# Post-norm attention and ternary feed-forward block on one core: the last seven tiles of the weight quantizer are quantized behind the projections, one a step, in other buffers

## The chip, the core and the metric

The kernel runs on one core of a Trainium2 chip. Its engines are PE (matrix multiply, with PEld for the loading of its weights), DVE (vector), ACT (scalar), POOL (GpSimd) and SP (which here only issues DMAs). Each engine works through its own list of instructions in order; semaphores tie the lists together. The metric is device time in microseconds. The kernel before takes 661.32 us (median of three runs, 660.82 to 663.54).

## The reference

Four sequences of 512 rows, model width 512, 16 query heads of 32 columns that share one key head and one value head, then a feed-forward part of hidden width 1408 whose three weights are first reduced to the values -1, 0 and 1:

```python
x = _layernorm(x + attn(x, Wq, bq, Wk, bk, Wv, bv, Wo, bo))   # rotary q, k; softmax; shared k, v
x = _layernorm(x + ffn(x, w1, w2, w3))

def _quantize(w):
    gamma = jnp.mean(jnp.abs(w))
    return jnp.clip(jnp.round(w / (gamma + EPS)), -1.0, 1.0)
def _bitlinear(x, w):
    return jnp.matmul(x, _quantize(w).T)
def ffn(x, w1, w2, w3):
    return _bitlinear(jax.nn.sigmoid(_bitlinear(x, w1)) * _bitlinear(x, w2), w3)
```

Everything is float32.

## The kernel before

**Steps.** The program is written as 64 steps, n = 0 to 63: sequence b = n // 16, column chunk c of 128 (four heads), row chunk t of 128 keys. A step emits, for its four heads, eight score matmuls (`ps`: four from `qT` and `kT`, four that add the negated row maxima from `negm`), two exponentials on ACT (`es`), and the weighing of the step before (`acc`). For b > 0 POOL adds up the exponentials (`total`, four additions for each step with t > 0). Seven steps ahead (`LEAD = 7`) the row maxima of a later head are found: PE makes `pmax`, DVE reduces it to `maxima`; `spread` turns a chunk's maxima into `negm` by two small DMAs of SP (`rows<-m`, then two of `negm<-rows`).

**Filler.** What else PE has to do is drawn into the steps by `fill.draw`: the projections of the next sequences (`project_in`: `pk`, `pq`), the output projection (`project_out`: `po`, then the transposes `pt`, which DVE splits into `y`), and the feed-forward part (`feed_forward`: `gu`, `hw`, `h`, `po`). As long as projections are left (`batches[-1].done < NC`, up to step 25) a step takes the first branch of the loop, after that the second one.

**Quantizing.** `quantized()` is a generator of 66 jobs; `quantize(k)` runs k of them. The matrices w1, w2, w3 have eleven tiles of 128x512 each. A first pass over a matrix sums absolute values on ACT (`junk`), a second one writes the ternary tile: ACT makes `sgn` (bfloat16), DVE makes the result in place (`raw<-raw,hi,sgn`), POOL stores it to DRAM (`kept`, in the profile `w<-raw`). POOL also issues the loads (`raw<-in_wf`), four jobs ahead; a store is issued two jobs behind its job. Jobs 55 to 65 are the second pass over w3. Three jobs stand in each of the seven leading steps, two in each of steps 0 to 15, and one or two in each step from 16 on, so that job 65 falls in step 25.

**Buffers.** `raw` lies in the rings `wg` (4 buffers, even jobs) and `wd` (5 buffers, odd jobs) of `wp`. The feed-forward part later loads its weights into the same rings (`load_weight`, loads `wg<-w` and `wd<-w` on SP), and takes a buffer when its last user is through, a store to DRAM included. `xT`, the transposed input, has a ring of 6 buffers in `work`. `sgn` lies in the ring `th` (2 buffers, later that of the gate's `th`) up to step 16, and after it in `rot_a`, a single buffer.

**Order.** Every engine call goes through `tc.keep_in_program_order`, so each engine's list is in the order in which the steps emit. SP's list holds the weights' loads, the heads' loads (`qr<-qp`), and the small DMAs for `negm` and for the denominators (`parts`, `few`, `flat`, `rden`), one behind the other.

Of the kernel before, what the change touches and what calls it, by code (L numbers as in the profile page):

```python
# [10 lines left out]
F32 = mybir.dt.float32  # L11
F32R = mybir.dt.float32r
BF16 = mybir.dt.bfloat16
# [7 lines left out]
P = 128  # L21
# [7 lines left out]
def postln_block(  # L29
# [22 lines left out]
    W = 512  # L52
# [4 lines left out]
    work = ctx.enter_context(tc.tile_pool(name="work", bufs=2))  # L57
    xp = ctx.enter_context(tc.tile_pool(name="xp", bufs=8))
    hp = ctx.enter_context(tc.tile_pool(name="hp", bufs=8))
    wp = ctx.enter_context(tc.tile_pool(name="wp", bufs=4))  # L60
# [16 lines left out]
    act, dve, pool = InOrder(nc.scalar), InOrder(nc.vector), InOrder(nc.gpsimd)  # L77

    def mm(out, lhsT, rhs, start, stop):
        pin(nc.tensor.matmul(out, lhsT=lhsT, rhs=rhs, start=start, stop=stop))  # L80

    def move(out, in_):
        pin(nc.sync.dma_start(out=out, in_=in_))
# [70 lines left out]


    kept = [[dram.tile([P, W], F32R, name=f"w{m}_{f}") for f in range(NF)] for m in range(3)]

    def quantized():

        order = ((0, False), (1, False), (0, True), (2, False), (1, True), (2, True))
        jobs = [(m, last, f) for m, last in order for f in range(NF)]

        means = {}
        for n, (m, last) in enumerate(order):
            if not last:
                for k, step in ((2, 0), (6, 1), (10, 2)):
                    means[(n + 1) * NF + k] = (m, step)
        raws, part, row, pg, hi, waiting = {}, {}, {}, {}, {}, []  # L170

        def load(k):
            if k < len(jobs):
                m, _, f = jobs[k]

                tag, bufs = ("wd", 5) if k % 2 else ("wg", 4)
                raws[k] = wp.tile([P, W], F32, tag=tag, name="raw", bufs=bufs)
                pool.dma_start(out=raws[k], in_=wf[m, f])

        def mean(m, step):  # L180
            if step == 0:
                row[m] = small.tile([P, 1], F32, tag="row", name="row")
                dve.tensor_reduce(row[m], part[m], AX.X, ALU.add)
            elif step == 1:
                pg[m] = ps_mm.tile([P, 1], F32, tag="mm", name="pg")
                mm(pg[m], ones, row[m], True, True)
                gamma = small.tile([P, 1], F32, tag="gamma", name="gamma")
                act.activation(gamma, pg[m], AF.Identity, scale=1.0 / (NF * W * P), bias=eps_q)
                row[m] = gamma
            else:  # L190
                hi[m] = small.tile([P, 1], F32, tag="hi", name="hi")
                act.mul(hi[m], row[m], 0.5)

        AHEAD = 4
        for k in range(AHEAD):
            load(k)
        for k, (m, last, f) in enumerate(jobs):
            load(k + AHEAD)
            if k in means:
                mean(*means[k])  # L200
            raw = raws.pop(k)
            if not last:
                if f == 0:
                    part[m] = small.tile([P, NF], F32, tag="part", name="part", bufs=3)
                junk = work.tile([P, W], BF16, tag="th", name="junk")
                act.activation(junk, raw, AF.Abs, accum_out=part[m][:, f : f + 1])
            else:
                if now > PER:

                    sgn = work.tile([P, W], BF16, tag="rot_a", name="sgn", bufs=1)  # L210
                else:
                    sgn = work.tile([P, W], BF16, tag="th", name="sgn")
                act.activation(sgn, raw, AF.Sign, bias=hi[m])
                dve.scalar_tensor_tensor(raw, raw, hi[m], sgn, ALU.is_gt, ALU.min)
                waiting.append((kept[m][f], raw))
            if len(waiting) > 2 or k + 1 == len(jobs):
                for w, q in waiting[: 1 if k + 1 < len(jobs) else 3]:
                    pool.dma_start(out=w.bitcast(F32), in_=q)
                del waiting[:1]
            yield  # L220

# [124 lines left out]
    def load_q(b, c):  # L346
        q = batches[b].q[c] = work.tile([P, T], F32, tag="qT", name="qT", bufs=3)
        move(q, batches[b].qd[c][0])
# [65 lines left out]
    def scores(b, c, t):  # L414
        s = batches[b]
        pss = []
        for j in range(2):
            ps = ps_sc.tile([P, 2, T], F32, tag="sc", name="ps")
            pss.append(ps)
            for i in range(2):  # L420
                rows = ts(2 * j + i, HD)
                mm(ps[:, i, :], s.kT[rows, ts(t, P)], s.q[c][rows, :], True, False)
        for j, ps in enumerate(pss):
            for i in range(2):
                rows = slice(HD * (2 * j + i), HD * (2 * j + i) + 2)
                mm(ps[:, i, :], ones_r[rows, :], s.negm[c][rows, :], False, True)
        es = []
        for j, ps in enumerate(pss):
            e = esp.tile([P, 2, T], F32, tag="es", name="es")
            act.activation(e, ps, AF.Exp, scale=SCALE)  # L430
            es.append(e)
        if b > 0:

            if t == 0:
                s.first = es
            elif t == 1:
                s.total = [work.tile([P, 2, T], F32, tag=f"total{j}", name="total", bufs=1) for j in range(2)]
                for j in range(2):
                    for i in range(2):
                        pool.tensor_tensor(  # L440
                            s.total[j][:, i, :], s.first[j][:, i, :], es[j][:, i, :], ALU.add
                        )
            else:
                for j in range(2):
                    for i in range(2):
                        pool.tensor_tensor(
                            s.total[j][:, i, :], s.total[j][:, i, :], es[j][:, i, :], ALU.add
                        )
        return es
# [130 lines left out]
        dve.tensor_tensor(tail, whole, head.bitcast(F32), ALU.subtract)  # L580

    def load_weight(m, f):
        tag, bufs = ("wd", 5) if m == 2 else ("wg", 4)
        w = wp.tile([P, W], F32R, tag=tag, name=tag, bufs=bufs)
        move(w.bitcast(F32), kept[m][f].bitcast(F32))
        return w
# [200 lines left out]
    def quantize(n):  # L787
        for _ in range(n):
            next(weights, None)

    steps = [(b, c, t) for b in range(B) for c in range(NC) for t in range(NT)]
    PER = NC * NT
# [5 lines left out]
    now = -1  # L798
# [3 lines left out]
    def due():  # L802

        nonlocal slot
        slot += 1
        for entry in list(late):
            if slot >= entry[0] and next(entry[1], "end") == "end":
                late.remove(entry)

    def begin_middle():  # L810
        late.extend(middle)
        middle.clear()
# [31 lines left out]
    def feed(b):  # L844
        fill.urgent.append(project_out(b))
        yield
# [18 lines left out]
    for n, (b, c, t) in enumerate(steps):  # L865
        now = n
        pace = (1.8, 3.8, 4.8, 4.6)[b]
        if t == 1 and PER <= n + NT - 1 < len(steps):
            load_q(*steps[n + NT - 1][:2])
        es = scores(b, c, t)  # L870
        if last is not None:
            weigh(*last)
        if last is not None and last[0] == 0:
            count(*last)
        last = (b, c, t, es)
        if n == NC * NT // 2:

            late.append((slot, load_x(0)))
        if t == NT - 1:
            begin = slot + 3  # L880
            late.append((begin, normalize(b, c)))
            if c == NC - 1:
                late.append((begin + 7, feed(b)))
                if b > 0:
                    late.append((slot + 6, load_x(b)))
        if batches[-1].done < NC:

            if b == 0:
                find_maxima(n + LEAD, 0, 1)
                begin_middle()  # L890
                due()
                find_maxima(n + LEAD, 2, 3)
            else:
                find_maxima(n + LEAD, 0)
                find_maxima(n + LEAD, 1, 2)
                find_maxima(n + LEAD, 3)
                begin_middle()
                due()
            quantize(1)
            fill.draw(pace)  # L900
            quantize(1 if b == 0 or n % 3 == 0 else 0)
        else:
            find_maxima(n + LEAD, 0)
            fill.draw(0.4 * pace)
            find_maxima(n + LEAD, 1, 2)
            begin_middle()
            due()
            fill.draw(0.3 * pace, True)
            find_maxima(n + LEAD, 3)
            fill.draw(0.3 * pace)  # L910
        due()
    weigh(*last)
    now = len(steps)
# [68 lines left out]
```

## Time and profile before

| what | us |
|---|---|
| median of the runs (lowest, highest) | 661.32 (660.82, 663.54) |
| the profiled execution's own time | 659.87 |
| its span, first to last instruction | 658.1 |
| PE busy | 635.4 (97%) |
| DVE busy | 440.3 (67%) |
| POOL busy | 327.4 (50%) |
| ACT busy | 282.6 (43%) |

The profile is of one execution. "Busy" is the time in which an engine has an instruction under way; the idle time in front of an instruction is put down to what released it. The chain of waits follows the work that ended last back to its start. The table by stretch gives each engine's busy time between two moments of the span, and the timeline gives the instructions of one engine in order of time; in it a number of instructions in a row is merged (x8), and a bracket tells the idle time before them and what ended it. In the span, step 16 begins at about 149 us, step 26 at 224.0, step 27 at 232.7, step 28 at 238.4, step 29 at 245.4, step 30 at 252.6, step 31 at 259.7, step 32 at 266.7 and step 33 at 275.6.

### The profile page before, as it was taken

The page shows a single profiled execution, that of the slowest core. Times are in us where ns is not written, and L with a number is a line of the kernel's source. Part 1 is how long each engine was busy: PE and PEld are TensorE (multiplying, and loading weights), DVE is VectorE, ACT ScalarE, POOL GpSimd, SP SyncE. Part 2 cuts the span into 40 slices and gives each one's busy share as a digit, 9 for nine tenths or more (in the row PEclk, how much of TensorE's full clock was granted, in tenths as well). Part 3 has the DMA queues.
Part 4 walks back from the last instruction along what each step waited for, and adds up shares of the span by engine and source line. Part 5 has one row for each costly group of instructions (what it writes and reads, how often), then busy time and mean ns, then how long its engine had stood idle before and what let it go on. Part 6 is the DMA issues. An engine that isn't in the chain of part 4 may idle for free.

```text
span 658.1 us, 9358 instructions
## 1 busy us (share of the span) xinstructions
PE 635.4 (97%) x3194; PEld 357.2 (54%) x3194; DVE 440.3 (67%) x629; ACT 282.6 (43%) x441; POOL 327.4 (50%) x416
## 2 busy tenths in 40 slices
PE   8999999999999999999999899999998999999995
PEld 5233333443333356665555566655555685778884
DVE  3987765787998977676666867667536544364335
ACT  2474656564454645333244354333454521234213
POOL 2434344545998766467666275576575703202000
PEclk9999999999999999999999999999999999999998
DMA  8946669788676286464132457541131473237531
GB/s 265 316 164 209 204 194 273 230 254 259 171 238 205 89 250 190 136 191 147 46 106 77 117 163 219 158 143 44 55 116 52 145 236 120 81 112 229 175 109 64
DMA packets 60671, 107.78 MB, mean 164 GB/s; under 512 B 14592, under 2 KB 15360, under 8 KB 60624
## 3 DMA queue, kind: packets, MB, share of 16 engines
q1 hardware_dynamic: 51984, 80.57, 40.2%
q0 software_dynamic: 7920, 25.96, 12.3%
q10 hardware_dynamic: 720, 0.66, 0.4%
q8 instruction: 25, 0.41, 0.3%
q14 instruction: 22, 0.18, 0.1%
HBM read 84.06 MB, written 23.10 MB: 163 GB/s over the span
## 4 chain that ended last, share of the span: by engine, by line
PE 85%; DVE 9%; ACT 4%; issue 2%; POOL 0%; DVEq 0%; ACTq 0%; POOLq 0%
PE gu L80 24%; PE po L80 19%; PE ps L80 13%; PE pmax L80 9%; PE acc L80 7%; PE pq L80 7%; DVE maxima L75 3%; ACT es L75 2%; PE den L80 2%; PE pk L80 2%; DVE part L75 1%; DVE xt L75 1%; DVE y L75 1%; DVE st L75 1%; PE warm L80 1%
## 5 line engine op out<-in xcount | busy, mean ns | idle before, releaser
L75 DVE TENSOR_REDUCE maxima<-pmax 128x1 f32<-128x512 f32 (+1 forms) x169 | 157.8, 955 | 69.9 <-PE pmax L80 69.7
L75 ACT ACTIVATE es<-ps 128x1024 f32<-128x1024 f32 x128 | 124.2, 1021 | 117.6 <-PE ps L80 116.7
L80 PE MATMUL gu<-y,wg 128*128 128x512 f32 x704 | 171.6, 393 | 0.1
L80 PEld LDWEIGHTS gu<-y,wg 128*128 128x128 f32 x704 | 131.7, 188 | 33.7 <-issue 4.9
L75 POOL TENSOR_TENSOR total<-total,es 128x512 f32<-128x512 f32 x96 | 125.2, 1336 | 38.5 <-ACT es L75 38.3
L80 PE MATMUL po<-wd,h 128*128 128x512 f32 x352 | 86.5, 394 | 3.3 <-DVE y L75 2.9
L75 POOL TENSOR_TENSOR total<-es 128x512 f32<-128x512 f32 x48 | 60.9, 1302 | 52.5 <-ACT es L75 52.5
L80 PE MATMUL pmax<-kr,qr 128*128 128x512 f32 x192 | 74.7, 452 | 3.2 <-DVE maxima L75 1.0
L80 PEld LDWEIGHTS po<-wd,h 128*128 128x128 f32 x352 | 65.1, 188 | 20.8 <-DVE y L75 4.6
L75 ACT CAST h<-hw 128x512 fp32r<-128x512 f32 x44 | 27.3, 620 | 103.0 <-DVE hw L75 103.0
L80 PE MATMUL acc<-es,v 128*32 128x512 f32 x512 | 68.2, 605 | 0.0
L80 PEld LDWEIGHTS pmax<-kr,qr 128*128 128x128 f32 x192 | 34.6, 188 | 55.9 <-issue 17.0
L75 DVE SCALAR_TENSOR_TENSOR hw<-th,gu 128x512 f32<-128x512 f32 x44 | 30.2, 686 | 44.3 <-PE gu L80 43.1
L80 PE MATMUL po<-wo_sb,ctxT 128*128 128x512 f32 x128 | 58.8, 592 | 0.0
L75 DVE TENSOR_TENSOR h<-hw,h 128x512 fp32r<-128x512 f32 x44 | 44.2, 1005 | 21.7 <-ACT h L75 21.4
L80 PE MATMUL ps<-negm,ones_r 2*128 2x512 f32 x256 | 58.7, 788 | 0.0
L75 DVE SCALAR_TENSOR_TENSOR xt<-po,xt 128x512 f32<-128x512 f32 x48 | 32.8, 684 | 37.0 <-PE po L80 37.0
L80 PE MATMUL ps<-qT,kT 32*128 32x512 f32 x384 | 56.3, 640 | 0.0
L75 POOL DMA_DIRECT2D raw<-in_wf x66 | 36.0, 548 | 38.1 <-DMA w<-raw 27.2
L80 PE MATMUL pq<-xT,wq_sb 128*128 128x512 f32 x112 | 53.1, 602 | 0.9 <-ACT v L75 0.9
L75 ACT ACTIVATE th<-gu 128x512 f32<-128x512 f32 x44 | 26.3, 597 | 49.9 <-PE gu L80 49.8
L80 PEld LDWEIGHTS po<-wo_sb,ctxT 128*128 128x128 f32 x128 | 24.1, 189 | 21.2 <-issue 19.2
(99 smaller groups left out, 640.2 us busy)
## 6 DMA issues: line engine op xcount, KB each, us to landing
wg<-w SPq DMA_DIRECT2D x88, 256.0 KB
raw<-in_wf POOLq DMA_DIRECT2D x66, 256.0 KB, 4.6
qr<-qp SPq DMA_DIRECT2D x96, 128.0 KB
wd<-w SPq DMA_DIRECT2D x44, 256.0 KB
w<-raw POOLq DMA_DIRECT2D x33, 256.0 KB, 4.6
qp<-q SPq DMA_DIRECT2D x48, 128.0 KB
rden<-flat SPq DMA_DIRECT2D x64, 64.0 KB
xt<-in_x SPq DMA_DIRECT2D x16, 256.0 KB
```

What stands on the lines that cost most here:

```text
L75: return lambda *args, **kw: pin(getattr(self.engine, name)(*args, **kw))
L80: pin(nc.tensor.matmul(out, lhsT=lhsT, rhs=rhs, start=start, stop=stop))
```

## The change

The last seven jobs (59 to 65) get buffers of the ring `xT`, which the projections leave one by one, and their loads are issued two jobs ahead in place of four. While projections are left, sequence 1 quantizes one tile in every second step; after them, one tile in each step. The signs always lie in the ring `th`. `load_weight` makes sure that a tile was stored before its load is emitted.

```diff
+    LATE = 7
+    stored = set()
...
-                tag, bufs = ("wd", 5) if k % 2 else ("wg", 4)
-                raws[k] = wp.tile([P, W], F32, tag=tag, name="raw", bufs=bufs)
+                if k >= len(jobs) - LATE:
+                    raws[k] = work.tile([P, W], F32, tag="xT", name="raw", bufs=6)
+                else:
+                    tag, bufs = ("wd", 5) if k % 2 else ("wg", 4)
+                    raws[k] = wp.tile([P, W], F32, tag=tag, name="raw", bufs=bufs)
...
-            load(k + AHEAD)
+            if k + AHEAD < len(jobs) - LATE:
+                load(k + AHEAD)
+            elif k + 2 >= len(jobs) - LATE:
+                load(k + 2)
...
-                if now > PER:
-
-                    sgn = work.tile([P, W], BF16, tag="rot_a", name="sgn", bufs=1)
-                else:
-                    sgn = work.tile([P, W], BF16, tag="th", name="sgn")
+                sgn = work.tile([P, W], BF16, tag="th", name="sgn")
...
     def load_weight(m, f):
+        while (m, f) not in stored:
+            quantize(1)
...
                 begin_middle()
                 due()
-            quantize(1)
+            quantize(1 if b == 0 or n % 2 == 0 else 0)
             fill.draw(pace)
-            quantize(1 if b == 0 or n % 3 == 0 else 0)
+            quantize(1 if b == 0 else 0)
         else:
...
             begin_middle()
             due()
+            quantize(1)
             fill.draw(0.3 * pace, True)
```

The stored tiles are also entered in `stored` where POOL's store is emitted.

More of the change, by code (lines that the diff above doesn't have):

```diff
@@ L207, in quantized @@
             else:
-                if now > PER:
-                    sgn = work.tile([P, W], BF16, tag="rot_a", name="sgn", bufs=1)
-                else:
-                    sgn = work.tile([P, W], BF16, tag="th", name="sgn")
+                sgn = work.tile([P, W], BF16, tag="th", name="sgn")
                 act.activation(sgn, raw, AF.Sign, bias=hi[m])
                 dve.scalar_tensor_tensor(raw, raw, hi[m], sgn, ALU.is_gt, ALU.min)
-                waiting.append((kept[m][f], raw))
+                waiting.append((m, f, raw))
             if len(waiting) > 2 or k + 1 == len(jobs):
-                for w, q in waiting[: 1 if k + 1 < len(jobs) else 3]:
-                    pool.dma_start(out=w.bitcast(F32), in_=q)
+                for m, f, q in waiting[: 1 if k + 1 < len(jobs) else 3]:
+                    pool.dma_start(out=kept[m][f].bitcast(F32), in_=q)
+                    stored.add((m, f))
                 del waiting[:1]
```

## The prediction

> **What bounds the kernel now.** I read the page first: busy times, and the chain that ended last.
>
> ```profile
> PE 635.4 (97%) x3194; PEld 357.2 (54%) x3194; DVE 440.3 (67%) x629; ACT 282.6 (43%) x441; POOL 327.4 (50%) x416
> PE 85%; DVE 9%; ACT 4%; issue 2%; POOL 0%; DVEq 0%; ACTq 0%; POOLq 0%
> ```
>
> PE is the bound, so a gain can only come out of its 22.7 us of idle time (658.1 - 635.4). The table by stretch shows how much of that lies where the change works. Columns: length, then busy time (and instructions) of PE, PEld, DVE, ACT, POOL, then granted clock, DMA share, GB/s.
>
> ```profile
> 187.30:202.00 14.70, 14.32 (x66) 5.62 (x65) 14.27 (x18) 6.09 (x8) 13.46 (x15) 1.00 0.88 290
> 224.00:232.70 8.70, 6.39 (x41) 3.27 (x40) 7.94 (x14) 5.49 (x9) 8.68 (x9) 1.00 0.60 178
> 232.70:238.40 5.70, 5.58 (x37) 2.81 (x36) 4.37 (x7) 2.70 (x4) 5.63 (x6) 1.00 0.84 267
> 245.40:252.60 7.20, 7.20 (x42) 4.49 (x41) 6.02 (x8) 3.24 (x5) 4.59 (x4) 1.00 1.02 293
> ```
>
> Up to step 25 DVE is full (14.27 of 14.70), yet PE idles 0.4 us in two steps. Only step 26 (224.0 to 232.7) loses time: 2.3 us. From step 27 on PE is full and DVE has 15 to 50% to spare. PE's timeline (start, length, engine, line, operation, in brackets the idle time before it and what ended it) gives the two waits of step 26, and the two matmul groups of step 28 that matter below:
>
> ```profile
> 229.20 0.66 PE L86 MATMUL pt<-ident,xt 128*128 128x128 f32 x4 [1.13 <-DVE q L75]
> 232.13 0.66 PE L86 MATMUL pt<-ident,xt 128*128 128x128 f32 x4 [1.07 <-DVE y L75]
> 238.36 1.14 PE L80 MATMUL ps<-qT,kT 32*128 32x512 f32 x8
> 238.92 0.81 PE L80 MATMUL ps<-negm,ones_r 2*128 2x512 f32 x4
> ```
>
> Last, the queues that the moved jobs pass, SP's and POOL's timelines:
>
> ```profile
> 232.36 1.51 SPq L83 DMA_DIRECT2D wg<-w  x3
> 233.92 1.08 SPq L83 DMA_DIRECT2D negm<-rows  x2
> 242.07 0.34 SPq L83 DMA_DIRECT2D wg<-w  x1
> ...
> 220.83 4.96 POOL L75 TENSOR_TENSOR total<-es 128x512 f32<-128x512 f32 x4 [2.88 <-ACT es L75]
> 225.75 1.74 POOL L75 TENSOR_TENSOR q<-q,q 128x512 fp32r<-128x512 f32 x1
> 227.43 1.63 POOL L75 DMA_DIRECT2D w<-raw  x3
> 229.07 4.96 POOL L75 TENSOR_TENSOR total<-total,es 128x512 f32<-128x512 f32 x4
> ```
>
> The third `wg<-w` (tile 1 of w1) starts at about 233.4, and `negm` for step 28 is directly behind it.
>
> **What moves.** Set side by side, the two programs have the same lists on PE and SP. DVE, ACT and POOL have the same work in another order: 13 jobs (53 to 65) in steps 16 to 25 become five there and eight (58 to 65) one a step in steps 26 to 33. A job is a sign (ACT 0.72), a `raw` operation (DVE) and two DMA issues (POOL 0.54 and 0.55).
>
> **Taken from steps 17 to 25.** Eight `raw` operations: 13 of them in this stage have a median of 1.22 us, so 9.8 us of DVE, and 8 x 1.09 = 8.7 us of POOL. PE's idle time from 155 to 215 is 1.5 us (60.0 - 58.5), put down to `es` and `v`, which stay; I take 0. In step 26 the wait of 1.13 goes: two `raw` (0.75 and 1.14, with 0.69 of waiting for a sign) no longer stand ahead of `q`, which ends some 2 us earlier. Late next is `y`: job 58's `raw` now stands ahead of the second `y`, against POOL's additions of step 26 (from 227.0 on). It costs 0.75 to 2.96 (the longest `raw`), so the fourth `pt` comes between 1 us sooner and 1 us later than 232.13. ACT's 8.8 us of waiting for the single sign buffer also goes; no PE wait hangs on it. Whatever is won here is lost in step 28, as follows.
>
> **The new wait.** Buffers decide it. Job 58 keeps a buffer of `wg` until its store, and jobs 54 and 56 were held longer too; so the third weight load, tile 1 of w1, gets the buffer of job 56 and waits for that job's store to land. Before, it waited for the store of job 62, issued at about 217. Now job 56's store is emitted with job 58, in step 26. In POOL's list it stands behind: `total` of step 25 (220.83 to 225.8), `q` (1.26, to 227.05), `total` of step 26 (4.96, to 232.0), `q` (1.26, to 233.3), one load's issue (0.56): 233.9. Landing from issue: 4.0 for the single store at 210 (DMA share 0.68), 2.5 in the quietest place (217), 6.0 in the fullest (139). I take 4.0, since the share of the stretch is between: 237.9. SP goes on at 238.0 in place of 233.4, 4.6 late. The second `negm` load starts at 234.45 + 4.6 = 239.05. Its landing: 1.85 (`flat` at 205.12 to `rden` at 206.97) and 2.45 (`rows` at 257.41 to `negm` at 259.86) are SP's waits for such small transfers; at most 3.9, since before it was issued by 235.0 and in use at 238.92. I take 2.45: 241.5, against 238.92: **+2.6**. Ends: 2.5 and 1.85 give 239.3, +0.4; 6.0 and 3.9 give 244.9, +6.0.
>
> The page "DMA: Bandwidth & Descriptors" of the Trainium skill, section "Anatomy of one DMA — SWDGE (gpsimd) path", fits 2.0 us plus bytes over 436 GB/s, which for 256 KB would be an estimated 2.6 us, against the 4.0 measured here; by it the wait would be 1.2 us.
>
> Behind `negm` on SP are `flat`, `qw`, `qp`, `qr`, `rden` and the next weight, tile 1 of w2: issued at 242.07 + 4.1 = 246.2 (SP stood idle for 0.5 at 235.0), there 3.7 later by the first weight (232.36 to 236.10), at 249.9; needed at 248.06 + 2.6 = 250.7. Covered by 0.8 us. `qr` is asked for three steps ahead.
>
> **Put into steps 27 to 33.** DVE's last `maxima` of a step has to end before the next step's first `pmax`: margins 0.54, 0.79, 0.62 and 0.63 us in steps 28 to 31 (ends 247.18, 254.11, 261.33, 268.38; `pmax` at 247.72, 254.90, 261.95, 269.01). A `raw` in front costs 0.75 alone, which passes these margins by 0.2, 0, 0.1 and 0.1; at the 1.22 of the busy stage by 0.7, 0.4, 0.6 and 0.6. Here `h` follows `raw`, and the timelines of DVE and POOL show that it already waits for POOL:
>
> ```profile
> 171.34 2.96 DVE L75 SCALAR_TENSOR_TENSOR raw<-raw,hi,sgn 128x512 f32<-128x512 f32 x1
> 168.82 4.94 POOL L75 TENSOR_TENSOR total<-total,es 128x512 f32<-128x512 f32 x4
> 259.01 1.79 DVE L75 TENSOR_TENSOR h<-hw,h 128x512 fp32r<-128x512 f32 x1
> ```
>
> The first ends 0.54 after POOL's four additions (173.76), having waited through two of them. `raw` will now do `h`'s waiting, so it should add little above 0.75. Ends 0.4 and 2.3; I take **+0.9**. The signs (0.72) fall in ACT's idle time (over 3 us a step); loads are issued 7 us or more before their sign.
>
> The page "SBUF — State Buffer" of the Trainium skill, section "Who interferes with whom", gives the shared ports to whoever is first for one whole instruction; that would cap a `raw` at an estimated 0.75 + 1.25 = 2.0 us, and the 2.96 above is more. The rule speaks against putting `raw` beside POOL's additions; by its cap all eight would stay within the 2.3 above.
>
> **Sum.** 2.6 + 0.9 = +3.5: span 661.6, own time 659.87 + 3.5 = 663.4. The median of the runs before is 1.45 above the profiled execution, so 661.32 + 3.5 = **664.8**.
>
> **Rivals.** *The wait stays hidden* (22%): POOL's additions of step 26 start earlier because the stage before is lighter, the store lands in time, and the two waits of step 26 go, with the 0.4 us of step 25: -2.6, 658.7. For it: 9.8 us of DVE freed. Against it: those additions need `es` of step 26, which ends when PE lets it. It decides if SP starts the third `wg` by 235. Only if nearly all idle time of 155 to 233 goes (1.5 + 2.5 = 4.0) is it over 0.5%. *The queues pile up* (16%): the load of tile 3 of w1 gets job 58's buffer and waits for its store, which waits in POOL for `ctxT`, and that for `rden`, now late: `rden` out at 246.3, `ctxT` from 248.2 to 249.5, store at 250.0, landed at 254.0; SP is then 6.3 late, and `negm` for step 32 (issued by 260.9, needed at 267.27) is late from 7.0 on. With landings of 6.0: 3.5 + 2.0 + 1.3 = +6.8, 668.1. For it: the share of 1.02 at 245 to 252; against it: POOL's loads there are few.
>
> **Numbers.** A measurement here tells about 0.5%, 3.3 us, from no change. My forecast (62%) runs from +0.8 to about +7 with 3.5 chosen, so 36 points lie above 3.3 and 26 below. Slower: 36 + 16 = 52%. Faster: 10 of the first rival's 22 points, the other 12 within. Within: 26 + 12 = 38%. The range runs from 659.6, leaving out about half of the first rival, to 668.8, just above the second.
>
> **What would show it.** Right: SP waits several us for `w<-raw` before the third `wg`, and PE waits in step 28 for DMA `negm`; step 26 loses less than 2.3 us. Wrong: `negm` issued by 235, no idle PE in step 28; or more than 2 us of PE waits on `maxima` in steps 28 to 33, which would make DVE the cause.

## The result, and the profile after

The changed kernel takes 666.46 us (median of seven runs, 665.33 to 667.91) against 662.11 us for the kernel before beside it: ratio 1.0066, 95% interval 1.0048 to 1.0083, or +4.4 us (+3.2 to +5.5). Its profiled execution took 666.46 us with a span of 664.7 us. The two profiles are 6.6 us apart. The profile of before is an execution in which PE's granted clock stayed whole (1.00) through step 27; a second profile of the same kernel, below, shows half clock (0.50) there and is 2.8 us longer. So the medians price the change, and the profiles say where.

The page of the changed kernel, busy times and the chain that ended last:

```profile
PE 637.5 (96%) x3194; PEld 356.4 (54%) x3194; DVE 437.6 (66%) x629; ACT 282.2 (42%) x441; POOL 326.7 (49%) x416
PE 75%; DVE 9%; DMA 6%; ACT 3%; issue 2%; SPq 2%; POOL 2%; DVEq 0%; POOLq 0%; ACTq 0%
```

PE's share of the chain fell from 85 to 75%, and DMA, SP and POOL, which had none of it to speak of, now hold a tenth. PE idles 27.2 us in place of 22.7. The table by stretch (columns as before: length, PE, PEld, DVE, ACT, POOL, granted clock, DMA share, GB/s):

```profile
187.30:202.00 14.70, 14.33 (x67) 5.65 (x65) 11.11 (x16) 4.76 (x6) 9.15 (x8) 1.00 0.55 161
224.00:232.70 8.70, 5.74 (x40) 2.82 (x39) 8.02 (x13) 5.64 (x9) 8.70 (x7) 1.00 0.52 156
232.70:238.40 5.70, 5.70 (x30) 2.38 (x30) 3.80 (x8) 3.13 (x4) 4.69 (x6) 0.70 0.41 143
```

In steps 21 and 22 DVE lost 3.2 us and POOL 4.3 us of work, and PE did the same as before: nothing gained. In the stretch of step 26 PE is busy for less than before (5.74 in place of 6.39). And in that of step 27 the granted clock is 0.70, where it was 1.00 before. PE's timeline, and behind it SP's, give the places (start, length, idle time before and what ended it in brackets):

```profile
232.53 0.66 PE L86 MATMUL pt<-ident,xt 128*128 128x128 f32 x4 [2.67 <-DVE y L75]
234.95 1.94 PE L80 MATMUL acc<-es,v 128*32 128x512 f32 x8
241.33 0.51 PE L80 MATMUL ps<-negm,ones_r 2*128 2x512 f32 x4 [0.29 <-DMA negm<-rows]
258.46 0.50 PE L80 MATMUL pmax<-kr,qr 128*128 128x512 f32 x1 [0.93 <-DVE maxima L75]
262.08 2.08 PE L80 MATMUL gu<-y,wg 128*128 128x512 f32 x8 [0.82 <-DMA wg<-w]
300.33 2.11 PE L80 MATMUL gu<-y,wg 128*128 128x512 f32 x8 [1.15 <-DMA wg<-w]
...
230.69 7.72 SPq L83 DMA_DIRECT2D wg<-w  x3
238.45 1.08 SPq L83 DMA_DIRECT2D negm<-rows  x2
```

The wait of 1.13 for `q` is gone; the other one of step 26 grew from 1.07 to 2.67, and the matmuls behind it run slower (`acc` 1.94 in place of 1.07). `negm` comes at 241.33, where `ps` stood at 238.92 before. Then PE waits for maxima and, twice, for a weight. On SP the three loads `wg<-w` take 7.72 us where they took 1.51, 6.4 of it waiting for `w<-raw`, and `negm` is behind them. The chain of waits of the changed kernel from step 26 on (start, length, what):

```profile
234.74 3.29 DMA w<-raw
238.09 0.32 SPq L83
239.02 2.18 DMA negm<-rows
241.33 0.51 PE ps L80 x3
...
245.48 3.55 DMA rden<-flat
...
251.09 6.74 DMA w<-raw
257.85 4.10 DMA wg<-w
262.08 2.08 PE gu L80 x8
```

This is the chain of the forecast, and the one of its second rival right behind it: job 56's store, SP, `negm`; then `rden`, `ctxT`, job 58's store, tile 3 of w1.

The table shows by how much each step's first `ps` came later than in the first profile of before, in us, for all kernels told of here (before: step 26 at 223.97, 28 at 238.36, 29 at 245.43, 30 at 252.60, 31 at 259.65, 35 at 291.63, 36 at 298.69). Each row is one profile. Where more than 2 us are lost before step 26, a stretch of half clock at 49 us is among it; where step 28 comes 0.9 us or more later than step 26 did, one between 231 and 240 us is.

| kernel | 26 | 28 | 29 | 30 | 31 | 35 | 36 |
|---|---|---|---|---|---|---|---|
| before, second profile | 0.3 | 2.7 | 2.7 | 2.7 | 2.7 | 2.7 | 2.7 |
| changed | 0.6 | 1.6 | 2.1 | 2.6 | 4.7 | 4.8 | 6.5 |
| changed, second profile | 1.0 | 3.2 | 3.2 | 4.2 | 4.7 | 5.3 | 6.1 |
| stores sooner | 0.2 | 2.2 | 2.2 | 2.5 | 2.5 | 2.6 | 2.7 |
| job 58 behind `y` | 0.7 | -1.4 | 3.1 | 3.6 | 3.6 | 3.8 | 4.3 |
| no late `raw` | 2.6 | 0.5 | 5.2 | 5.2 | 5.2 | 5.7 | 5.7 |
| both edits | 2.0 | -0.1 | 1.8 | 2.6 | 2.6 | 2.7 | 4.0 |
| before, stores held | 0.5 | 0.1 | 1.6 | 1.7 | 1.7 | 1.6 | 1.6 |
| `raw` last | -0.1 | -2.2 | -1.6 | -1.4 | -1.4 | -1.4 | -1.4 |
| second store alone | 1.0 | 2.0 | 2.0 | 3.3 | 4.2 | 4.4 | 5.3 |
| stores sooner, covered | 0.4 | 0.1 | 0.1 | 2.0 | 2.0 | 2.1 | 3.7 |
| before, covered | -0.1 | 0.6 | 0.6 | 0.6 | 0.6 | 0.6 | 1.7 |
| signs alone | 1.5 | 1.6 | 1.6 | 1.6 | 1.6 | 1.6 | 1.6 |

### The profile page after: what moved, and what is told of

It reads as the page before. It is cut to its first block, busy times and chain, and to the rows that moved or that the text cites. A ratio compares the mean times of both kernels' runs of the same rounds, so it can differ in the third digit from the quotient of the medians.

```text
span 664.7 us, 9365 instructions
## 1 busy us (share of the span) xinstructions
PE 637.5 (96%) x3194; PEld 356.4 (54%) x3194; DVE 437.6 (66%) x629; ACT 282.2 (42%) x441; POOL 326.7 (49%) x416
## 4 chain that ended last, share of the span: by engine, by line
PE 75%; DVE 9%; DMA 6%; ACT 3%; issue 2%; SPq 2%; POOL 2%; DVEq 0%; POOLq 0%; ACTq 0%
PE gu L80 20%; PE po L80 19%; PE ps L80 11%; PE pmax L80 7%; PE acc L80 7%; PE pq L80 6%; DVE maxima L75 3%; SPq L83 2%; PE den L80 2%; ACT es L75 2%; DMA qr<-qp 2%; DMA w<-raw 2%; POOL total L75 1%; PE pk L80 1%; DMA wg<-w 1%
## 5 line engine op out<-in xcount | busy, mean ns | idle before, releaser
L75 DVE TENSOR_TENSOR h<-hw,h 128x512 fp32r<-128x512 f32 x44 | 40.5, 922 | 21.3 <-ACT h L75 21.0
```

The costliest lines, as they stand in the source:

```text
L75: return lambda *args, **kw: pin(getattr(self.engine, name)(*args, **kw))
```

## The experiments

Each kernel was timed against the kernel before on its own chip; differences between two kernels are differences of these ratios, times 662.5 us. The theory: late stores hold SP's queue, and PE waits for what stands behind them. Rival 1: `raw` is in the way on DVE, ahead of `y` and `maxima`, and the clock falls after the long wait. Rival 2: the moved traffic itself.

**Stores sooner.** The stores of jobs 56 to 65 go out one job behind, not two.

```diff
-            if len(waiting) > 2 or k + 1 == len(jobs):
-                for m, f, q in waiting[: 1 if k + 1 < len(jobs) else 3]:
...
-                del waiting[:1]
+            behind = 0 if k + 1 == len(jobs) else 1 if k >= 57 else 2
+            while len(waiting) > behind:
+                m, f, q = waiting.pop(0)
...
```

> The changed kernel, with the stores of jobs 56 to 65 issued one job behind in place of two; DVE, ACT, PE and SP keep their lists. The changed kernel is 4.35 us over the one before. Theory (late stores hold SP's queue): the third wg load no longer waits into 238, so the 0.29 us of PE waiting for negm in step 28 goes; the load of tile 3 of w1 no longer waits for a store landing at 257.8, so the 0.82 us of PE waiting for wg and the 2.1 us that step 30 lost go, and at most the 1.8 us of step 35 with them: 2.4 to 4.2 us faster than the changed kernel, 0 to +2 us against before. What stays is step 26's wait of 2.67 us for y and the half clock after it. Rival 1 (raw in the way of y and maxima on DVE, and the clock after it): within 0.5 us of the changed kernel, +4 against before. Rival 2 (the moved traffic itself slows the loads): within 1 us of the changed kernel, with wg still late in step 30.

Measured: 1.0011 (0.9992 to 1.0029), +0.7 us on before and 3.6 (2.0 to 5.3) less than the changed kernel, as the theory said. DVE's order and the moved traffic are those of the changed kernel, so neither rival can be the greater part of the loss by itself. SP's three loads `wg<-w` take 1.43 us again. What PE still waits for between 200 and 310 us of the span (total, times, longest, us):

```profile
PE pt L86 <- DVE y L75: 2.9, 2, 2.7
PE pmax L80 <- ACT es L75: 0.6, 3, 0.2
PE pmax L80 <- DVE maxima L75: 0.2, 1, 0.2
```

All waits for DMA are gone, and with them most of the wait for maxima in step 30. The wait for `y` stayed, and so did the half clock: the profile loses 2.1 us between steps 26 and 28 and 0.5 after that. The changed kernel lost 1.0 and 2.2 us there in its two profiles, and 5.0 and 2.9 after that. So by these profiles what the edit gives back lies behind step 28.

**Job 58 behind `y`.** The sign and `raw` of job 58 are emitted at the end of step 26; the stores that used to go with the job stay in the middle of the step.

```diff
             raw = raws.pop(k)
+            if k == 58:
...
+                yield
...
             fill.draw(0.3 * pace)
+            quantize(1 if n == PER + 10 else 0)
```

> The changed kernel, with the sign and the raw operation of job 58 emitted at the end of step 26, behind all four y; its stores and loads stay where they were. Theory (late stores hold SP's queue): step 26's wait for y falls from 2.67 to about 1 us and PE's clock stays whole in step 27, but negm of step 28 still lands at 241.3 and then binds alone, so step 28 starts no more than 0.3 us sooner: 0 to 1 us faster than the changed kernel, +3.4 to +4.4 against before; PE's wait for negm grows from 0.29 to about 2 us. Rival 1 (DVE's order and the clock): 2.0 to 3.5 us faster than the changed kernel, +1 to +2 against before.

Measured: 1.0038 (1.0020 to 1.0057), +2.5 us on before and 1.9 (0.2 to 3.5) less than the changed kernel, between what the theory and rival 1 had. The mechanism was the theory's: step 27 is whole, PE is three microseconds sooner at step 28, and there it waits for `negm`, until 240.74 in place of 241.33.

```profile
240.74 0.51 PE L80 MATMUL ps<-negm,ones_r 2*128 2x512 f32 x4 [2.02 <-DMA negm<-rows]
242.83 3.23 PE L80 MATMUL gu<-y,wg 128*128 128x512 f32 x8
```

The second line, a `gu` group that takes 2.0 otherwise, shows that the half clock now follows this wait. What is won comes after step 29: tile 3's load starts at 256.88 in place of 257.85, PE is 1 us later, and the wait for it in step 30 is gone.

**Both edits** of the two kernels above, put together (job 58's first half now issues all stores that wait: `len(waiting) > 0`).

> Both edits: stores from job 56 on one job behind, and the sign and raw of job 58 behind the four y of step 26. Theory: with the stores gone from SP's way and the y wait back to about 1 us, only the maxima waits of steps 29 to 31 (1.1 us more than before) stay, against 1.1 us less of waiting for q in step 26: -1 to +1 us against before. Rival 1 (DVE's order): +0.5 to +2, as in the run that moves job 58 alone. Rival 2 (the moved traffic itself): +3 or more, with wg late in step 30 again.

Measured: 1.0005 (0.9988 to 1.0021), +0.3 us on before, within the theory's range. With SP free and step 26 short, what is left in the profile is 1.9 us of waiting for maxima in steps 28 and 29 and 0.8 for a weight in step 35.

**Before, stores held.** The kernel before, with the last four stores held back to step 26. Nothing moves on DVE.

```diff
+            if len(waiting) > 2 and k < 64:
+                w, q = waiting.pop(0)
...
+        for w, q in waiting:
+            pool.dma_start(out=w.bitcast(F32), in_=q)
```

> The kernel before, with the stores of its last four jobs (62 to 65) held back to the end of step 26, and no job moved: DVE and ACT as before. The third wg load then waits for a store issued at about 233 to 234 and landed at about 237 to 238. Theory (the store's landing holds SP, and negm behind it): step 28's second four ps start 2.4 us later, at about 241.3 in place of 238.92, with PE's wait put down to negm: +1.5 to +3 us against before. Rival 1 (DVE's order and the clock): no raw stands ahead of y here, so 0 to +0.7. Rival 2 (the moved traffic): 0 to +0.7.

Measured: 1.0007 (0.9988 to 1.0027), +0.5 us (-0.8 to +1.8). The wait is there, behind SP's wait for a store, which ends at about 237.2:

```profile
240.81 0.50 PE L80 MATMUL ps<-negm,ones_r 2*128 2x512 f32 x4 [1.20 <-DMA negm<-rows]
```

and the profile loses 1.5 us in step 28 and nothing after it. But the times moved less than the theory asked, and do not part it from its rivals. Late stores that hold up `negm` of step 28 alone cost 1.8 us at most here, by the end of the interval; the 4.4 of the change are more than that.

**No late `raw`.** The changed kernel without DVE's `raw` from job 58 on, so that the last eight tiles are stored unquantized.

```diff
-                dve.scalar_tensor_tensor(raw, raw, hi[m], sgn, ALU.is_gt, ALU.min)
+                if k < 58:
+                    dve.scalar_tensor_tensor(raw, raw, hi[m], sgn, ALU.is_gt, ALU.min)
```

> The changed kernel without the raw operation on DVE for jobs 58 to 65 (the last eight tiles of w3 are stored unquantized); signs, loads and stores stay. Theory (late stores hold SP's queue, DVE adds the smaller part): step 26's wait for y falls to about 1 us, PE's clock stays whole in step 27 and the 0.9 us of waiting for maxima in step 30 goes, but negm still lands at about 241 in step 28 and then costs 1.5 to 2 us by itself: as in the run that moves job 58 alone, 1 to 2.5 us faster than the changed kernel, +2 to +3.5 against before. Rival 1 (raw on DVE is the cause): 3.5 to 4.5 us faster than the changed kernel, level with before.

Measured: 1.0044 (1.0024 to 1.0065), +2.9 us on before, 1.5 (-0.3 to 3.2) less than the changed kernel. Rival 1 as the whole cause falls: with none of these `raw` on DVE, most of the loss is still there, and it is where the theory puts it.

```profile
242.82 0.51 PE L80 MATMUL ps<-negm,ones_r 2*128 2x512 f32 x4 [2.81 <-DMA negm<-rows]
```

**Signs alone.** The kernel before with its signs in the ring `th`.

```diff
-                if now > PER:
...
-                    sgn = work.tile([P, W], BF16, tag="rot_a", name="sgn", bufs=1)
-                else:
-                    sgn = work.tile([P, W], BF16, tag="th", name="sgn")
+                sgn = work.tile([P, W], BF16, tag="th", name="sgn")
```

> The kernel before with the signs always in the ring th, and no job moved. Theory and rivals: ACT's 8.8 us of waiting for the single sign buffer goes, and no PE wait hangs on it: within 1 us of before. If it were slower by over 1 us, the change's own ring for the signs would be part of its cost.

Measured: 1.0003 (0.9978 to 1.0028). This part of the change costs and gains nothing that can be measured (at most 1.9 us to either side).

**Before, a second profile.**

> The kernel before, profiled a second time, to see how far one profile stands for the kernel: its runs lie between 660.2 and 665.7 us at mean granted clocks of PE from 0.998 to 0.989. Theory: steps 26 to 36 take the same times within 0.5 us, and what differs between runs is stretches of half clock after idle times of 1 us or more, 1 to 2 us each. Rival: step 26's own waits vary by over 1 us from run to run, and then no single profile can price them.

It took 662.68 us, 2.81 more than the first. The waits of step 26 are the same to 0.03 us, and step 27 is not (the last line is its stretch in the table, at clock 0.50):

```profile
229.54 0.66 PE L86 MATMUL pt<-ident,xt 128*128 128x128 f32 x4 [1.10 <-DVE q L75]
232.47 1.11 PE L86 MATMUL pt<-ident,xt 128*128 128x128 f32 x4 [1.07 <-DVE y L75]
232.70:238.40 5.70, 5.70 (x25) 2.05 (x25) 2.86 (x6) 2.52 (x3) 4.01 (x4) 0.50 0.80 267
```

The theory held, but for a size: half clock from 231.6 to 238.5 cost 2.4 us where it had 1 to 2, and steps 28 to 35 took the same times as in the first profile.

**The second store alone.** As "stores sooner", but from job 58 on only, so that the stores of jobs 56 and 57 stay late.

```diff
-            behind = 0 if k + 1 == len(jobs) else 1 if k >= 57 else 2
+            behind = 0 if k + 1 == len(jobs) else 1 if k >= 59 else 2
```

> The changed kernel with the stores one job behind only from job 58 on: job 56's store, which holds the third wg and negm of step 28, stays where the change put it, job 58's goes from step 28 to step 27, ahead of ctxT. Theory (the second late store is what makes the change slower than the forecast's own sum: step 30's first gu cannot start before 262.1 in either profile of the changed kernel, whatever PE lost before): SP still starts its third wg at about 238 and negm lands at about 241.3, but tile 3 of w1 is there 5 us sooner, and step 30 loses no more than 0.3 us to it: 1.5 to 2.5 us faster than the changed kernel, +2 to +3 against before. Rival 1 (DVE's order and the clock alone): within 0.5 us of the changed kernel. Rival 2 (the first store alone): within 0.5 us of the changed kernel too, with the loss of step 30 moved to a wait for maxima.

Measured: 1.0063 (1.0038 to 1.0088), 0.2 us less than the changed kernel (-1.8 to +2.2). The theory's 1.5 to 2.5 did not come, though the interval does not quite shut it out. The store went out at 244.2 in place of 251.1 and tile 3 was loaded from 249.41; but SP again waited until about 238.3, and `negm` came at 241.19, as late as in the changed kernel (PE, late itself, lost nothing by it). A weight was 0.47 late in step 29, and step 30 lost its time to maxima, as rival 2 had it:

```profile
259.11 0.50 PE L80 MATMUL pmax<-kr,qr 128*128 128x512 f32 x1 [0.82 <-DVE maxima L75]
```

"Stores sooner" moves the earlier stores too and is 3.4 us (1.4 to 5.5) faster than this. So the loss hangs on the first stores, those of jobs 56 and 57, and not on job 58's alone; in this profile other waits took the place of that one.

**Covered idle time.** Two kernels put matmuls that nothing reads where PE waits in step 26, to keep the clock whole.

```diff
+            for _ in range({2: 6, 3: 6}.get(t, 0) if b == 0 else 0):
...
+                mm(s.cover[:, 0, 0:P], ones, ones, True, True)
```

> The kernel before with twelve matmuls of 128x128 on ones, six ahead of each of the two transposes of step 26 that wait (1.1 us each), so that PE does not idle there; nothing reads them. Theory (the idle time of step 26 is what brings half clock in about half of the runs, 2.4 us in step 27 in the second profile of before): step 27 takes 5.7 us, the runs lose their upper part (664 to 666), and the median is 0.5 to 2 us under before. Rival (the clock falls of itself, whatever PE does): same median within 0.5 us, same spread of 5 us.

> The changed kernel with stores one job behind and fourteen such matmuls ahead of the last transpose of step 26, which waits 2.67 us for y; nothing reads them. Theory: the wait for y itself costs only 0.3 us more than step 26 lost before, and the half clock after it 1.8 us, so covering it makes this 1.5 to 2.5 us faster than the run with stores sooner alone, 0 to -1.5 against before. Rival 1 (the wait on DVE is the cost, not the clock): within 0.5 us of that run, +0.5 to +1.5.

Six of them stand ahead of each of the last two transposes in the kernel before, fourteen ahead of the last one in "stores sooner". In both profiles the clock is 1.00 from 226 to 240. Both expectations of the time were missed. The kernel before with the cover: 1.0015 (0.9989 to 1.0040). The edit was off: the first six stand one transpose behind the wait for `q`, which stayed (1.08), and six take 1.50 us, more than the wait; steps 26 and 27 together grew by 0.6 us, and three of twelve runs still lay above 665. It tells little of the clock. "Stores sooner" with the cover: 1.0035 (1.0011 to 1.0058), not sooner than without. Its step 28 is on time (+0.1), and then PE waits for weights that it had been too late to wait for:

```profile
252.18 2.11 PE L80 MATMUL gu<-y,wg 128*128 128x512 f32 x8 [1.30 <-DMA wg<-w]
297.81 2.11 PE L80 MATMUL gu<-y,wg 128*128 128x512 f32 x8 [1.31 <-DMA wg<-w]
```

The load of 252.18 stood on SP behind the one that waits for job 58's store until 247.75. So in this profile what a whole clock saved in step 27 went into these two waits.

**The changed kernel, a second profile.** 

> The changed kernel, profiled a second time. Theory: the wait for y of about 2.7 us with half clock after it, negm at 241 to 242 and the late store of job 58 with the wait for wg in step 30 come again within 0.7 us each, since each follows from the order of the lists; step 35's 1.8 us comes from when SP's small transfers land and may be gone. Rival: the wait for wg in step 30 is gone or under 0.5 us, and then late stores are no fixed cost of this order.

It took 666.05 us. The wait for `y` (2.65), the half clock and SP's wait until 238.5 came again. But the clock stayed down for twice as long, step 28 started 3.2 us late, PE no longer waited for `negm`, and the wait for tile 3 in step 30 was 0.26. The rival's mark was reached, and yet that `gu` starts at 262.15, where it started at 262.08 in the first profile: PE's own delay and the store's end at the same time, and the shorter one hides behind the other.

**`raw` last.** Both edits, and from step 26 on each step's sign and `raw` behind its last maxima.

```diff
-            if k == 58:
-                while len(waiting) > 0:
+            if k >= 58:
+                while waiting:
...
-            quantize(1 if n == PER + 10 else 0)
+            quantize(1)
```

> The version with both edits, and in every step from 26 on sign and raw of the step's job emitted at the step's end, behind its last maxima; stores and loads stay in the middle of the step. Theory: the 1.9 us that PE waited for maxima in steps 28 and 29 goes, the wait of 1.1 for y in step 26 stays, and no store holds SP: 0.5 to 2 us faster than the version with both edits, -2 to 0 us against before. Rival 1: raw only moves its harm to the first maxima or to h of the next step: level with the version with both edits.

Measured: 660.67 us, 0.9975 (0.9951 to 0.9999), -1.7 us against before and 2.0 less than with both edits. What PE waits for between 200 and 310 us:

```profile
PE pt L86 <- DVE y L75: 1.3, 2, 1.1
PE pmax L80 <- ACT es L75: 0.5, 3, 0.2
```

No wait for maxima, `negm` or weights is left, and step 36 stands 1.4 us sooner than before. This version is the fastest of all here; its interval only just leaves out no change.

## Why the prediction was right, and where it was not

*The direction and the cause* were right: late stores hold SP's queue, and moving them alone gives 3.6 of the 4.4 us back. The forecast had job 56's store out at 233.9, landed at 237.9, `negm` at 241.5; the profile has 234.74, 238.03 and 241.33. POOL was 0.8 later (the additions of step 26 took 5.41 against 4.96 and began 0.5 later) and the store 0.7 shorter. The next weight went out at 246.0 against 246.2. The Trainium skill's fit ("DMA: Bandwidth & Descriptors", "Anatomy of one DMA — SWDGE (gpsimd) path"), by an estimate 2.6 us for 256 KB, is below the 3.3 of this store and far below the 6.7 of job 58's.

*But the 2.6 us are not all the wait's own.* In the first profile `negm` bound PE at 241.33, 2.4 us later than before; half of that had been lost in step 27, and PE idled for `negm` for 0.29 us only, in the second profile not at all. Where the wait stands alone, in the kernel before with stores held, step 28 lost 1.5. The step that failed is that on step 26: "the fourth `pt` comes between 1 us sooner and 1 us later than 232.13 ... Whatever is won here is lost in step 28". It came at 232.53, within that, but the two waits of 1.1 us became one of 0.30 and one of 2.67, and the clock that fell behind it cost step 27 1.1 us (steps 26 and 27 lost 2.2 in the second profile). The forecast had no term for the clock, and its sign that step 26 would lose less than 2.3 us did not come: PE idled there for 3.0. The two delays cover each other. From step 26 to step 29 the changed kernel lost 1.5 and 2.2 us in its two profiles, "stores sooner" 2.1, job 58 behind `y` 2.4, no late `raw` 2.6; both edits lost nothing there (-0.2). With the long wait for `y` gone, and the half clock of step 27 with it, PE waits for `negm` for 2.0 or 2.8 us instead.

*The +0.9 for `raw` in steps 27 to 33* was close in sum, not in place: 1.1 us of waits for maxima in the first profile, 0.9 in the second, nearly all of it in one step (30 and 29). `raw` does wait through POOL's additions, for as long as 2.93 us (at 254.28). That is more than the cap of 2.0 us of which the forecast speaks. Its remark that by this cap all eight stay within 2.3 does not follow from its own margins either: a `raw` of 2.0 us passes those of steps 28 to 31 by 5.4 us in sum.

*The second rival* (16%) was no rival but the continuation. Its store left at 251.09, 1.1 later than it had it, and landed after 6.74, where 4.0 was taken; it hit not `negm` of step 32 but the weight itself, two steps sooner. In the first profile step 30 lost 2.1 us, in the second 0.5. That moving the second store alone gave nothing back that could be measured fits the same picture: this is no sum of terms, since the forecast's, the rival's and DVE's delays overlap.

*The size:* 4.4 (3.2 to 5.5) against 3.5. "Stores sooner" gives 3.6 back, job 58 behind `y` 1.9, both 4.0. The first stores and what they set off are the greater part, but not where the forecast had it. The first profile lost 1.0 us in steps 26 and 27, 0.6 in step 28, 0.5 in 29, 2.1 in 30 and 1.8 in 35, where the sum had 2.6 in step 28 and 0.9 in steps 28 to 31. That the sum came so near is in part luck: the clock and the late weights, which the sum left out, made up for a wait that cost less. What stays open is the exact split, since each interval is about 1.7 us to either side, and step 35: its late weight (1.15 and 0.46 us in the two profiles) follows SP's `flat`, which comes 1 us later in the step than before with `raw` ahead of `few` on DVE; the profile with `raw` last no longer has the wait, and neither has the one without late `raw`, but in "stores sooner" and with job 58 behind `y` `flat` is as late and the wait is not there, and no run took that `raw` away alone. *The first rival* (a hidden wait) fell: SP's wait was 6.4 us and ended at 238, where the rival needed 235.

## What to carry to other kernels

When buffers are handed on from one use to the next, ask which store frees each of them and where that store stands in the issuing queue; a store that is two jobs behind becomes two steps late when jobs are spread one to a step. A wait on a queue of small transfers reaches all who stand behind it, and taking away one of several delays that end together shows only the next. Move the work behind the step's last due result, and its stores ahead of the next one: both together turned the loss of this change into a gain, if any, of 1.7 us (0.1 to 3.2).

## What the runs showed of the hardware

The granted clock of PE fell to 0.50 with every single wait of 2.0 to 2.8 us (six profiles of six: 2.67, 2.65, 2.66, 2.65, 2.02 and 2.81), at a moment between the wait itself and 1.3 us after its end, and stayed there for 3.4 us (four of them) or for 6.8 (two). With two waits of 1.1 us within 4 us it fell in one profile out of four (before twice, stores held, signs alone), there for 6.8 us, and behind one of 1.1 us that ends at 46.8 us in two of fourteen. Of 97 runs of the kernel before that stand beside the experiments, 44 had a mean clock of 0.995 or more and a median of 660.9 us, the others 663.3: apart by the 2.4 us that step 27 lost in the second profile. Whether all of this spread is step 26's stays open.

The page "TensorE: Matmul & The Clock Gate" of the Trainium skill, section "Part 1: The HAM clock gate", gives a free-running window of 3.4 us for this; the lengths 3.4 and 6.8 are one and two such windows. Its rule in "HAM oscillation — how this bites in real kernels", no idle gaps of more than about 3.4 us, is too mild here: 2.0 us was enough in every case seen.
